# Moving attention weights to their source row by the table's transfer instead of by 0/1 matmuls, in two outlook-attention layers

## The chip, the cores and the metric

The kernel runs on one core of one Trainium2 chip. The metric is the device time of one execution in microseconds; smaller is better. A profile of one execution goes with the times.

## The reference, cut to what matters

Two residual layers over an image batch `x` of shape (8, 56, 56, 384), float32 throughout. Layer 0 normalizes over groups of channels, forms values `v` and, for each pixel, head (12) and each of 9 output offsets `p`, a softmax over 9 input offsets `q`; it weighs the 3x3 neighbourhood of `v` with it, and adds the result for offset `p` onto the pixel at offset `p` (a fold). Layer 1 does the same with 6 heads and no fold.

```python
v_unf = patches.reshape(b, n, k2, heads, d)               # layer 0
attn = jax.nn.softmax(a * d ** (-0.5), axis=-1)           # (b, n, heads, p, q)
out = jnp.einsum('bnhpq,bnqhd->bnphd', attn, v_unf)
canvas = canvas.at[:, i:i + h, j:j + w].add(out[:, :, :, p])
x = x + canvas[:, pad:pad + h, pad:pad + w] @ Wo.T

a = jax.nn.softmax(a.reshape(B, H * W, heads, k * k), axis=-1)   # layer 1
y = jnp.einsum('bpKhd,bphK->bphd', patches, a)
x = x + y @ W_proj + b_proj
```

Seen from a destination pixel, layer 0 is a weighted sum over a 5x5 neighbourhood of source pixels (row offsets -2 to 2), and layer 1 one over a 3x3 neighbourhood. A weight is computed at one pixel's row and is needed at another's.

## The kernel before, in words

A tile has one image column of two images on its partitions: 112 rows (`R`). A pair of images is walked column by column, 4 pairs of 56 columns, so 224 steps in layer 0. Eight groups (`px`) of seven columns make a pair.

Layer 0, one step. `attend` multiplies one column of the normalized input `xn` by the attention weights `wa_t` (three `bank` tiles of 288 columns on TensorE), takes the maximum and subtracts on VectorE (L550, L551), takes Exp on ScalarE (L555), sums on VectorE (L567 to L573), and multiplies by the reciprocal on POOL (L574). A fourth `bank` tile makes `v`, which ScalarE copies (L562) and sends to a table in HBM, `vtab` (L317). `presum`, two steps later, adds on POOL (L593 to L597) the weights of neighbouring columns that meet at one source column, into `pre`. `fold`, three steps later, moves them between rows: `pre` has nine blocks (destination offset `pi` by source offset `qi`), and row offset e from 0 to 4 gathers those with e = pi + 2 - qi. For `qi` = 0 and 2 it multiplies by a 0/1 matrix, `shift`, of TensorE, into `pw`; ScalarE copies the rows e = 0 and 4, to which only one block contributes (L619), VectorE adds the block `qi` = 1, which stays in its row, to e = 1 to 3 (L620), both into the tile `wt`. One or two DMAs of ScalarE's queue (L625), one for each `px` group that the column belongs to, write `wt` to a table in HBM, `ztab`. Its lines are the rows; a line has a slot for each column, and in a slot five pieces of `ROW0` = 84 numbers, one for each e, with zeros around them.

For each group, `bands` reads `ztab` back on SP's queue into `z` (L329), in the form of matrices that a contraction needs, `rows_to_patches` reads `vtab` into `vp`, `contract` multiplies the two (`pc`), ScalarE copies `pc` to `yT` (L664), and `project_out` multiplies by `wo_t` (`po`).

Layer 1 goes by groups of seven columns, 32 in all. `wc_t` makes logits and values in one `bank` tile of 438 columns. The logits go out to a table and come back by rows, `weigh` and `share` make the softmax, and `move` shifts it between rows with three 0/1 matmuls of 126 columns (`pw1`, named `pw` in the profile), nine ScalarE copies into `wz` and one DMA to `ztab1`. `fetch` reads four pieces of `z`, then two of `vp`, on SP's queue, for contractions three steps later.

The order on each engine is partly fixed by the code (a wrapper keeps TensorE, SP, POOL and all of layer 1 in program order); in layer 0 a scheduler orders ScalarE and VectorE. In both layers `jobs` holds contractions and projections, and hands one out between matmuls of the step. [...]

The matrix `inside` holds ones, with zeros at the rows whose neighbour lies in another image.

Of the kernel before, what the change touches and what calls it, by code (L numbers as in the profile page):

```python
# [8 lines left out]
F32 = mybir.dt.float32  # L9
AF = mybir.ActivationFunctionType  # L10
# [5 lines left out]
def two_outlook_layers(  # L16
# [32 lines left out]
    nc = tc.nc  # L49
# [5 lines left out]
    R = IMG * H  # L55
    MARGIN = 2
# [8 lines left out]
    PX = 7  # L65
    NPX = W // PX
# [3 lines left out]
    HEADS0, HEADS1 = 12, 6  # L70
    D0, D1 = C // HEADS0, C // HEADS1
    K, K2 = 3, 9
    E0 = 2 * K - 1
# [9 lines left out]
    ROW0 = HEADS0 * PX  # L83
    WT = 2 * SX0 - E0
    PY1, NPY1, SX1, SY1 = 8, 7, PX + 2, 10
    ROW1 = HEADS1 * PX
# [8 lines left out]
    EP1, FIRST1 = 11, 4  # L95
    SLOT0, SLOT1 = EP0 * ROW0, EP1 * ROW1
    LINE0, LINE1 = SX0 * SLOT0 + ROW0, SX1 * SLOT1 + ROW1
    NTAB = 3
# [11 lines left out]
    ztab0 = [dram.tile([RT + 1, LINE0], F32, name=f"ztab0_{n}") for n in range(NTAB)]  # L110
# [7 lines left out]
    def matmul(*args, **kwargs):  # L118
        tc.keep_in_program_order(nc.tensor.matmul(*args, **kwargs))  # L119
# [48 lines left out]
    shift = const.tile([R, K, R], F32, name="shift")  # L168
    gpsimd.memset(shift, 0.0)
    for k in range(-1, 2):  # L170
        s = shift[:, k + 1, :]
# [10 lines left out]
    inside = const.tile([R, K, PH_ALL], F32, name="inside")  # L182
# [12 lines left out]
    def fill(table, first, dims, width):  # L195

        src = zeros[: dims[0][1], :width]
        if len(dims) > 1:
            src = src.unsqueeze(1).to_broadcast([dims[0][1], dims[1][1], width])
        tc.keep_in_program_order(  # L200
            nc.sync.dma_start(bass.AP(table.tensor, table.offset + first, [*dims, [1, width]]), src)
        )
# [12 lines left out]
    def clear_weights(table, line, part, sx, slot, row, first, e, ep):  # L215
        fill(table, 0, [[part, MARGIN * line // part]], part)
        fill(table, (MARGIN + R) * line, [[part, (MARGIN + 1) * line // part]], part)
        top = MARGIN * line
        fill(table, top, [[line, R]], first * row)
        fill(table, top + (first + e) * row, [[line, R], [slot, sx]], (ep - e) * row)  # L220

    def clears():

        yield 3, lambda: clear_v(vtab0, SX0, 2)

        yield 4, lambda: fill(
            ztab0[0], MARGIN * LINE0 + FIRST0 * ROW0, [[LINE0, R], [SLOT0, 2]], E0 * ROW0
        )
        for n, t in enumerate(ztab0):
            yield (5, 2 * PX, 3 * PX)[n], lambda t=t: clear_weights(  # L230
                t, LINE0, 366, SX0, SLOT0, ROW0, FIRST0, E0, EP0
            )
        yield 4 * PX, lambda: clear_v(vtab1, SX1, 1)
        for n, t in enumerate(ztab1):
            yield (5 + n) * PX, lambda t=t: clear_weights(
                t, LINE1, 350, SX1, SLOT1, ROW1, FIRST1, K, EP1
            )
# [59 lines left out]
    def patches_of(col, pad):  # L297

        for px in range(NPX):
            sx = col - PX * px + pad  # L300
            if 0 <= sx < PX + 2 * pad:
                yield px, sx
# [51 lines left out]
    ps = ctx.enter_context(tc.tile_pool(name="ps", bufs=1, space=PS))  # L354
# [42 lines left out]
    def layer0(late, pools):  # L397
# [209 lines left out]
        def fold(pair, c):  # L607


            pre = pres.pop((pair, c)).rearrange("r (pi qi) f h -> r pi qi (f h)", qi=K)  # L610
            pw = ps.tile([R, E0, E0 * HEADS0], F32, tag="f", name=f"pw_{pair}_{c}")
            for qi in (0, 2):
                matmul(
                    pw[:, 2 - qi : 2 - qi + K, :], shift[:, qi, :], pre[:, :, qi, :],
                    start=(qi == 0), stop=(qi == 2), skip_group_check=True,
                )
            wt = wts[c % NWT]
            mid = wt[:, :, SX0 - E0 : SX0, :].rearrange("r e f h -> r e (f h)")
            nc.scalar.copy(mid[:, 0 : E0 : E0 - 1, :], pw[:, 0 : E0 : E0 - 1, :])  # L619
            nc.vector.tensor_tensor(mid[:, 1 : 1 + K, :], pw[:, 1 : 1 + K, :], pre[:, :, 1, :], ALU.add)  # L620

            for px, sx in patches_of(c, 2):
                lo = SX0 - 1 - sx
                at = sx * SLOT0 + FIRST0 * ROW0
                nc.scalar.dma_start(  # L625
                    ztab0[(pair * NPX + px) % NTAB][MARGIN : MARGIN + R, at : at + E0 * ROW0].rearrange("r (e w) -> r e w", e=E0),
                    wt[:, :, lo : lo + PX, :].rearrange("r e m h -> r e (m h)"),
                )

        def fetch_v(pair, px):  # L630
# [119 lines left out]
        for step in range(NPAIR * W + LAG):  # L750
            if 2 <= step < NPAIR * W + 2:
                presum(*divmod(step - 2, W))
            todo = [lambda: jobs.run(step, 1)] * 2
            if step >= LAG:
                todo.insert(1, lambda: fold(*divmod(step - LAG, W)))
            between = lambda: todo.pop(0)() if todo else None
            if step < NPAIR * W:
                attend(*divmod(step, W), between)
                upkeep(step)
            while todo:  # L760
                between()

            pair, c = divmod(step - LAG - PX, W)
            if pair >= 0 and c % PX == 0:
                fetch_v(pair, c // PX)
            pair, c = divmod(step - LAG - PX - 1, W)
            if pair >= 0 and c % PX == 0:
                fetch(pair, c // PX, step + 4)
# [15 lines left out]
    def layer1(pools, base, last_of_layer0, late_w):  # L784
        vector, scalar, sync = (InOrder(e) for e in (nc.vector, nc.scalar, nc.sync))
# [53 lines left out]
        NW = SX1 * K * ROW1  # L839
# [68 lines left out]

        def move(g):

            at = lgs.pop(g)

            pw = ps.tile([R, K, PX, K, HEADS1], F32, tag="f", name=f"pw1_{g}")
            for ki in range(K):
                matmul(
                    pw[:, K - 1 - ki].rearrange("r x f h -> r x (f h)"),
                    shift[:, ki, :],
                    at.rearrange("r x (i j) h -> r x i (j h)", j=K)[:, :, ki, :],
                    start=True, stop=True,
                )  # L920

            wz = wzs[g % 2]
            step = K * ROW1 + 1
            for kj in range(K):
                dst = wz[:, kj * K * ROW1 : kj * K * ROW1 + PX * step].rearrange("r (m e) -> r m e", e=step)
                dst = dst[:, :, : K * ROW1].rearrange("r m (e h o) -> r e m h o", e=K, h=HEADS1)
                for e in range(K):
                    scalar.copy(dst[:, e, :, :, 0], pw[:, e, :, kj, :])
            table = ztab1[g % NTAB]
            scalar.dma_start(  # L930
                bass.AP(
                    table.tensor, table.offset + MARGIN * LINE1 + FIRST1 * ROW1,
                    [[LINE1, R], [SLOT1, SX1], [1, K * ROW1]],
                ),
                wz[:, :NW].rearrange("r (s e) -> r s e", s=SX1),
            )

        def fetch(g, due):
            pair, px = divmod(g, NPX)
# [76 lines left out]
        for step in range((NG + 1) * PX):  # L1016
            g, m = divmod(step, PX)
# [3 lines left out]
            read, first, second, moved = (0, 2, 3, 4) if last else (1, 3, 4, 5)  # L1021
# [10 lines left out]
            if g and m == moved:  # L1032
                move(done)
# [69 lines left out]
```

## Time and profile before

| what | value |
|---|---|
| three runs, median (lowest to highest) | 3531.84 us (3530.87 to 3535.32) |
| the profiled execution's own time | 3516.74 us |
| its span, mean granted TensorE clock | 3514.6 us, 0.987 |
| layer 0's steps, first to last `pw` | 82.5 to 2311.5 us |
| layer 1's groups, first to last `pw` | 2392.0 to 3460.3 us |
| busy: TensorE, VectorE, POOL, ScalarE | 98%, 55%, 34%, 33% |
| DMA | 839.34 MB, mean 239 GB/s |

A span goes from the first to the last instruction; the time of the execution has a little around it. A row of the groups by shape reads: line, engine, operation, output<-inputs, shape, how often; then busy time in all, mean of one in ns, the engine's idle time before it and what ended that. The line of a helper stands for all its callers: L119 is every matmul, L132 whatever layer 1 keeps in order. A waits row names who waited, for whom, total us, times, and the longest. A DMA row ends with the median time from issue to landing.

### The profile page before, as it was taken

The page shows a single profiled execution, that of the slowest core. Times are in us where ns is not written, and L with a number is a line of the kernel's source. Part 1 is how long each engine was busy: PE and PEld are TensorE (multiplying, and loading weights), DVE is VectorE, ACT ScalarE, POOL GpSimd, SP SyncE. Part 2 cuts the span into 40 slices and gives each one's busy share as a digit, 9 for nine tenths or more (in the row PEclk, how much of TensorE's full clock was granted, in tenths as well). Part 3 has the DMA queues.
Part 4 walks back from the last instruction along what each step waited for, and adds up shares of the span by engine and source line. Part 5 has one row for each costly group of instructions (what it writes and reads, how often), then busy time and mean ns, then how long its engine had stood idle before and what let it go on. Part 6 is the DMA issues. An engine that isn't in the chain of part 4 may idle for free. (4 is left out here: it accounts for less than half of the span.)

```text
span 3514.6 us, 72311 instructions
## 1 busy us (share of the span) xinstructions
PE 3427.7 (98%) x29014; PEld 2353.0 (67%) x29014; DVE 1935.8 (55%) x4680; ACT 1173.3 (33%) x2727; POOL 1202.1 (34%) x1833
## 2 busy tenths in 40 slices
PE   7899999999999999999999999988999999999998
PEld 5577777777777777777777777655666666666665
DVE  6666666667666676667766666633333333333331
ACT  4333223333333233333322223223434434343432
POOL 2543434434344344344443444331222222221220
PEclk8999999999999999999999999999999999999998
DMA  8999988688886878887757776676878787878775
GB/s 270 286 288 282 275 275 267 212 256 253 279 263 209 272 221 273 259 252 256 236 181 226 245 225 193 222 271 192 226 221 234 217 229 219 243 205 237 216 219 147
DMA packets 672893, 839.34 MB, mean 239 GB/s; under 512 B 302190, under 2 KB 566574, under 8 KB 668462
## 3 DMA queue, kind: packets, MB, share of 16 engines
q1 hardware_dynamic: 321422, 537.46, 47.9%
q10 hardware_dynamic: 323872, 210.54, 22.7%
q0 software_dynamic: 27264, 86.73, 7.5%
q8 instruction: 228, 3.74, 0.5%
q14 instruction: 107, 0.88, 0.1%
HBM read 512.95 MB, written 321.66 MB: 237 GB/s over the span
## 5 line engine op out<-in xcount | busy, mean ns | idle before, releaser
L119 PE MATMUL bank<-wa_t,xn 128*112 128x288 f32 x4032 | 1086.9, 409 | 11.4 <-ACT v L562 7.8
L574 POOL TENSOR_TENSOR at<-at,den 112x972 f32<-112x972 f32 x224 | 504.6, 2253 | 1193.1 <-DVE den L573 1137.8
L119 PEld LDWEIGHTS bank<-wa_t,xn 128*112 128x112 f32 x4032 | 693.4, 177 | 263.7 <-issue 34.3
L119 PE MATMUL po<-yT,wo_t 128*128 128x448 f32 (+1 forms) x2304 | 817.5, 494 | 5.3 <-DVE x1t L685 4.8
L119 PEld LDWEIGHTS po<-yT,wo_t 128*128 128x128 f32 x2304 | 432.8, 191 | 293.5 <-issue 185.4
L119 PE MATMUL pc<-z,vp 121*32 121x49 f32 (+1 forms) x17664 | 487.9, 254 | 25.3 <-DMA vp<-vtab 10.4
L119 PEld LDWEIGHTS pc<-z,vp 121*32 121x32 f32 (+1 forms) x17664 | 441.3, 131 | 103.3 <-issue 79.5
L550 DVE TENSOR_REDUCE mx<-bank 112x36 f32<-112x324 f32 x672 | 327.6, 487 | 310.6 <-PE bank L119 303.7
L317 POOL DMA_DIRECT2D vtab<-v x392 | 213.1, 547 | 825.3 <-DVE v L132 810.4
L119 PE MATMUL bank<-wc_t,xn 128*128 128x438 f32 x1176 | 478.8, 543 | 5.0 <-DMA wo_t<-in_wo 5.0
L119 PE MATMUL bank<-wv_t,xn 128*128 128x384 f32 x1176 | 417.9, 492 | 0.0
L555 ACT ACTIVATE at<-at 112x972 f32<-112x972 f32 x224 | 227.0, 1014 | 344.9 <-DVE at L551 317.6
L551 DVE TENSOR_TENSOR at<-bank,mx 112x324 f32<-112x324 f32 x672 | 328.8, 489 | 21.1 <-DVE mx L550 0.5
L119 PEld LDWEIGHTS bank<-wc_t,xn 128*128 128x128 f32 x1176 | 214.0, 191 | 174.8 <-issue 162.4
L119 PEld LDWEIGHTS bank<-wv_t,xn 128*128 128x128 f32 x1176 | 219.5, 190 | 139.6 <-issue 18.7
L619 ACT COPY wt<-pw 112x120 f32<-112x120 f32 x224 | 58.0, 259 | 654.0 <-PE pw L119 591.2
L597 POOL TENSOR_TENSOR pre<-at,at 112x108 f32<-112x108 f32 (+1 forms) x440 | 238.0, 541 | 110.4 <-DVE wt L620 96.0
L567 DVE TENSOR_TENSOR d<-at 112x432 f32<-112x432 f32 x224 | 141.7, 632 | 204.7 <-ACT at L555 204.7
L132 DVE TENSOR_TENSOR lgt<-bank,ba_t 128x54 f32<-128x54 f32 x196 | 41.7, 213 | 361.3 <-PE bank L119 361.3
L132 DVE SCALAR_TENSOR_TENSOR x1t<-po,bo_t,x1t 128x448 f32<-128x448 f32 (+1 forms) x156 | 97.7, 626 | 248.9 <-PE po L119 248.9
L664 ACT COPY yT<-pc 128x294 f32<-128x294 f32 x256 | 103.4, 407 | 368.9 <-PE pc L119 325.9
L535 ACT ACTIVATE xn<-xin,bias,scale 128x224 f32<-128x224 f32 x336 | 172.9, 566 | 67.2 <-PE bank L119 36.0
(100 smaller groups left out, 2924.6 us busy)
## 6 DMA issues: line engine op xcount, KB each, us to landing
z<-ztab SPq DMA_DIRECT2D x64, 2352.0 KB, 18.0
vp<-vtab SPq DMA_DIRECT2D x64, 1536.0 KB, 8.3
ztab<-wt ACTq DMA_DIRECT2D x336, 183.8 KB, 6.8
vp<-vtab SPq DMA_DIRECT2D x64, 945.0 KB, 12.0
xres<-xT SPq DMA_DIRECT2D x32, 1176.0 KB, 10.1
xin<-xT ACTq DMA_DIRECT2D x54, 672.0 KB, 7.3
z<-ztab SPq DMA_DIRECT2D x128, 258.4 KB, 4.5
x1t<-x SPq DMA_DIRECT2D x26, 1176.0 KB, 19.0
```

The source lines that it names most:

```text
L119: tc.keep_in_program_order(nc.tensor.matmul(*args, **kwargs))
L132: return lambda *args, **kwargs: tc.keep_in_program_order(op(*args, **kwargs))
L317: queue.dma_start(bass.AP(table.tensor, table.offset + first, [[line, rows], [(R + GAP) * line - PX * C, n], [1, C]],), v.unsqueeze(1).to_ ...
L535: nc.scalar.activation(to[:, i, :, rows], xin[:, i, :, rows], AF.Identity, bias=bias[:, i, b : b + 1], scale=scale[:, i, b : b + 1],)
L550: nc.vector.tensor_reduce(mx[:, pi, :], pl.rearrange("r q a -> r a q"), AX.X, ALU.max)
L551: nc.vector.tensor_tensor(at[:, pi], pl, mx[:, pi, :].unsqueeze(1).to_broadcast([R, K2, PH]), ALU.subtract)
L555: nc.scalar.activation(at, at, AF.Exp, scale=SCALE0)
L567: nc.vector.tensor_add(d4, at[:, :, 0:4], at[:, :, 4:8])
L574: nc.gpsimd.tensor_tensor(at, at, den.unsqueeze(2).to_broadcast([R, K, K2, PH]), ALU.mult)
L597: nc.gpsimd.tensor_tensor(dst, terms[0], terms[1], ALU.add)
L619: nc.scalar.copy(mid[:, 0 : E0 : E0 - 1, :], pw[:, 0 : E0 : E0 - 1, :])
L664: nc.scalar.copy(yT[:, :, :, b, rows_of], pc.rearrange("p i n y m -> p i m (n y)"))
```

## The change

Row offsets 0 and 4 of layer 0, and all three of layer 1, are no longer moved by TensorE. ScalarE scales the block in its own row by a column of `inside` (zero where the destination lies outside the image) and writes it to `wt` or `wz`; the DMA to the table adds a whole number of lines to the address, so that it lands on the destination's row. In layer 0 the 0/1 matmuls stay for offsets 1 to 3, where two or three blocks are summed: each takes two blocks instead of three, 120 columns instead of 180. The one DMA of five pieces becomes one of three pieces (offsets 1 to 3) and one of two (0 and 4). In layer 1 the one DMA of 126 numbers a slot becomes three of 42 (`ROW1`). Each table gets two more pieces cleared, in the lines that the shifted writes leave out.

```diff
@@ clear_weights
         fill(table, top + (first + e) * row, [[line, R], [slot, sx]], (ep - e) * row)
+        fill(table, top + first * row, [[slot, sx]], row)
+        fill(table, top + (R - 1) * line + (first + e - 1) * row, [[slot, sx]], row)
@@ fold, layer 0
             for qi in (0, 2):
+                lo = qi // 2
                 matmul(
-                    pw[:, 2 - qi : 2 - qi + K, :], shift[:, qi, :], pre[:, :, qi, :],
+                    pw[:, 2 - qi + lo : 4 - qi + lo, :], shift[:, qi, :], pre[:, lo : lo + 2, qi, :],
                     start=(qi == 0), stop=(qi == 2), skip_group_check=True,
                 )
...
-            nc.scalar.copy(mid[:, 0 : E0 : E0 - 1, :], pw[:, 0 : E0 : E0 - 1, :])
+            for e, pi, qi in ((0, 0, 2), (E0 - 1, 2, 0)):
+                nc.scalar.activation(
+                    mid[:, e, :], pre[:, pi, qi, :], AF.Copy, scale=inside[:, qi, 0:1]
+                )
             nc.vector.tensor_tensor(mid[:, 1 : 1 + K, :], pw[:, 1 : 1 + K, :], pre[:, :, 1, :], ALU.add)
...
                 nc.scalar.dma_start(
-                    ztab0[(pair * NPX + px) % NTAB][MARGIN : MARGIN + R, at : at + E0 * ROW0].rearrange("r (e w) -> r e w", e=E0),
-                    wt[:, :, lo : lo + PX, :].rearrange("r e m h -> r e (m h)"),
+                    bass.AP(table.tensor, first + ROW0, [[LINE0, R], [ROW0, K], [1, ROW0]]),
+                    weights[:, 1 : 1 + K],
+                )
+                nc.scalar.dma_start(
+                    bass.AP(
+                        table.tensor, first + LINE0,
+                        [[LINE0, R], [(E0 - 1) * ROW0 - 2 * LINE0, 2], [1, ROW0]],
+                    ),
+                    weights[:, 0 : E0 : E0 - 1],
                 )
@@ move, layer 1
-            pw = ps.tile([R, K, PX, K, HEADS1], F32, tag="f", name=f"pw1_{g}")
-            for ki in range(K):
-                matmul(
-                    pw[:, K - 1 - ki].rearrange("r x f h -> r x (f h)"),
-                    shift[:, ki, :],
-                    at.rearrange("r x (i j) h -> r x i (j h)", j=K)[:, :, ki, :],
-                    start=True, stop=True,
-                )
+            at = at.rearrange("r x (i j) h -> r i x j h", j=K)
...
-                for e in range(K):
-                    scalar.copy(dst[:, e, :, :, 0], pw[:, e, :, kj, :])
+                for ki in range(K):
+                    scalar.activation(
+                        dst[:, K - 1 - ki, :, :, 0], at[:, ki, :, kj, :], AF.Copy,
+                        scale=inside[:, ki, 0:1] if ki != 1 else 1.0,
+                    )
             table = ztab1[g % NTAB]
-            scalar.dma_start(
-                bass.AP(
-                    table.tensor, table.offset + MARGIN * LINE1 + FIRST1 * ROW1,
-                    [[LINE1, R], [SLOT1, SX1], [1, K * ROW1]],
-                ),
-                wz[:, :NW].rearrange("r (s e) -> r s e", s=SX1),
-            )
+            for e in range(K):
+                scalar.dma_start(
+                    bass.AP(
+                        table.tensor,
+                        table.offset + (MARGIN + 1 - e) * LINE1 + (FIRST1 + e) * ROW1,
+                        [[LINE1, R], [SLOT1, SX1], [1, ROW1]],
+                    ),
+                    wz[:, :NW].rearrange("r (s e w) -> r e s w", s=SX1, e=K)[:, e],
+                )
```

In the built program TensorE has 448 calls of `pw` at 120 columns where it had 448 at 180, and none of `pw1`; ScalarE has 448 scaled copies into `wt` for 224 copies, 288 into `wz` as before, 672 DMAs to `ztab` in layer 0 for 336, and 96 to `ztab1` for 32. The order of TensorE and of SP is otherwise the same, and POOL's nearly so; the scheduler orders ScalarE and VectorE anew in layer 0.

More of the change, by code (lines that the diff above doesn't have):

```diff
@@ L624, in fold @@
                 at = sx * SLOT0 + FIRST0 * ROW0
+                table = ztab0[(pair * NPX + px) % NTAB]
+                first = table.offset + MARGIN * LINE0 + at
+                weights = wt[:, :, lo : lo + PX, :].rearrange("r e m h -> r e (m h)")
                 nc.scalar.dma_start(
-                    ztab0[(pair * NPX + px) % NTAB][MARGIN : MARGIN + R, at : at + E0 * ROW0].rearrange("r (e w) -> r e w", e=E0),
-                    wt[:, :, lo : lo + PX, :].rearrange("r e m h -> r e (m h)"),
+                    bass.AP(table.tensor, first + ROW0, [[LINE0, R], [ROW0, K], [1, ROW0]]),
[7 more added lines that the diff above has]
+                    weights[:, 0 : E0 : E0 - 1],
                 )
```

## The prediction, made before the result was known

> **What bounds the kernel now.** I read the page's busy shares first, then the table by stretches of time, then the groups kept apart by shape, then the timeline around one column of layer 0 and one group of layer 1, and last the DMA issues. The page's shares and slices:
>
> ```profile
> PE 3427.7 (98%) x29014; PEld 2353.0 (67%) x29014; DVE 1935.8 (55%) x4680; ACT 1173.3 (33%) x2727; POOL 1202.1 (34%) x1833
> ...
> PE   7899999999999999999999999988999999999998
> ...
> DMA  8999988688886878887757776676878787878775
> ```
>
> TensorE is the only engine near its limit, in nearly every slice. Two rows of the table by stretches (length; busy us of PE, PEld, DVE, ACT, POOL; clock; DMA share; GB/s) show one late stretch of each layer:
>
> ```profile
> 1500.00:2300.00 800.00, 798.22 (x6985) 567.81 (x6987) 542.01 (x1314) 234.74 (x455) 330.88 (x481) 1.00 0.72 230
> 2430.00:2930.00 500.00, 499.28 (x3797) 311.82 (x3796) 157.79 (x335) 200.79 (x585) 110.89 (x205) 1.00 0.81 225
> ```
>
> PE idles 1.8 of 800 us and 0.7 of 500 us. Busy is not peak, so I set it against streaming: the timeline below shows matmuls that start as far apart as their columns cost, without holes. Hence a microsecond taken from PE's stream in either layer is a microsecond of the run, unless another engine then falls behind. The groups that the change touches, by shape:
>
> ```profile
> L119 PE MATMUL pw<-pre,shift 112*112 112x180 f32 x896 | 174.5, 316 | 10.2 <-POOL pre L595 10.2
> ...
> L619 ACT COPY wt<-pw 112x120 f32<-112x120 f32 x224 | 58.0, 259 | 654.0 <-PE pw L119 591.2 <-DMA vtab<-v 36.2 <-DMA xin<-xT 10.5
> ...
> L119 PE MATMUL pw<-at,shift 112*112 112x126 f32 x192 | 29.7, 290 | 0.0
> ```
>
> The means of 316 and 290 ns hold the pipeline's latency, and do not price a matmul. Starts do:
>
> ```profile
> 1012.04 0.78 PE L119 MATMUL pw<-pre,shift 112*112 112x180 f32 x4
> ...
> 1012.65 1.62 PE L119 MATMUL bank<-wa_t,xn 128*112 128x288 f32 x6
> ...
> 2529.38 0.91 PE L119 MATMUL pw<-at,shift 112*112 112x126 f32 x6
> ...
> 2530.12 0.49 PE L122 MATMUL bank<-ident,x1t 128*112 128x128 f32 x3
> ```
>
> Four instructions from 1012.04 to 1012.65 are 0.61 us, 152 ns each for 180 columns; six from 2529.38 to 2530.01 (the next weight load, PE's next work) are 0.63 us, 105 ns each for 126. Both are 0.84 ns a column.
>
> [...]
>
> **The change, part by part.** Times are against the profiled execution, 3516.7 us (span 3514.6); the median of the runs, 3531.8, is 15.1 us above it, and I carry that over unchanged.
>
> Layer 0, PE. `fold` makes 224 x 2 calls, 896 instructions; each falls from 180 to 120 columns. At 0.84 ns a column that is 101 ns instead of 152: 896 x 51 ns = **46 us** off PE. Could weight loads keep the old spacing? The same 112 x 112 weights already go in at 105 ns in layer 1, so 101 to 105: 42 to 46 us. PE's order is otherwise unchanged.
>
> Layer 1, PE. 192 instructions of 105 ns go: **20 us**. So 62 to 66 us leave PE; I take 66.
>
> Layer 0, ScalarE. One 112x120 copy (259 ns) becomes two 60-column activations with a scale per partition: [...], so +0.3 us a column. ScalarE also issues 336 more table DMAs, 1.5 a column, at 0.35 to 0.6 us (two issues of L625 take 0.95): +0.6 us. That is 0.9 us in a column of 9.95 us (2230 us over 224), on an engine 29% busy in the stretch 1500 to 2300. Its throughput hides it. Its order does not, wholly. The old copy waited for PE's matmul; the new activations wait for POOL's `pre`. And in the new order they stand, in most columns, ahead of the Exp two columns later, while the middle rows' DMA, which waits for VectorE's add, is issued after the next column's activations in 142 of 224 columns. So a ring closes: Exp, VectorE's denominator, POOL's product and `pre`, ScalarE's activations and issues, next Exp. One turn as it runs today:
>
> ```profile
> 1015.43 1.01 ACT L555 ACTIVATE at<-at 112x972 f32<-112x972 f32 x1 [2.32 <-DVE at L551]
> ...
> 1017.03 0.59 DVE L567 TENSOR_TENSOR d<-at 112x432 f32<-112x432 f32 x1
> ...
> 1020.08 2.25 POOL L574 TENSOR_TENSOR at<-at,den 112x972 f32<-112x972 f32 x1 [5.59 <-DVE den L573]
> ...
> 1023.13 0.27 POOL L595 COPY pre<-at 112x108 f32<-112x108 f32 x1
> ...
> 1026.12 1.02 ACT L555 ACTIVATE at<-at 112x972 f32<-112x972 f32 x1 [2.32 <-DVE at L551]
> ```
>
> `pre` is complete at 1023.40 and the next Exp starts at 1026.12: 2.7 us. The new ScalarE work in between is 0.5 us for the pair of activations and about three issues of 0.35, 1.55 us. Over columns 30 to 215, taken one by one from the trace, that gap averages 1.6 us, is under 1.55 in about four of ten, and below zero in two. So Exp often comes one to three microseconds later. Queued behind it are the copies of `v` and `yT`; VectorE's sums wait for it, and PE for VectorE's and ScalarE's release of the three banks. Three banks are some 4 us of PE work, so most of the lateness is absorbed. Bounds: 0 lost, if lateness never exceeds 4 us; or 36 us, if it is carried whole from turn to turn and only what exceeds 4 us stops PE. I take 15 us.
>
> Layer 0, DMA. The packets stay at five of 336 bytes a row, so bytes and packets are unchanged. [...]
>
> ```profile
> z<-ztab SPq DMA_DIRECT2D x64, 2352.0 KB, 18.0
> ...
> ztab<-wt ACTq DMA_DIRECT2D x336, 183.8 KB, 6.8
> ...
> ztab<-wz ACTq DMA_DIRECT2D x32, 496.1 KB, 4.4
> ```
>
> Today ScalarE loses about 95 us to DMA waits of up to 5.5 us and PE hardly notices; I expect 50 to 80 us more there and price it on PE at 3 us (0 to 15). SP's order is the same but for 12 small fills at the tables' clearing: nothing, among fills already there.
>
> Layer 0, VectorE. The add drops its wait for the copy (16.5 us in all) and is no longer: nothing.
>
> Layer 1, the move. Nine copies (0.99 us) become nine activations, six with a scale per partition: [...]. They no longer wait for `pw`, and start 0.4 us earlier. One table DMA becomes three, so the last issue is some 1.2 us later; 63 packets per DMA engine become 189. ScalarE's queue took 25 ns a packet in this stretch (55,408 packets, 8.2% of 16 x 1060 us), so landing is 1.5 (at 17 ns, as for the 216-byte packets of the same queue) to 2.8 us later. SP waits for it with z, and vp and x1t are queued behind z. The first vp lands at 2549.7 and its contraction begins at 2553.9: 4.2 us, less 0.6 that PE gains, less 1.5 to 2.8: 0.8 to 2.1 us left. So nothing, but each microsecond beyond it would cost 31 groups x 1 us.
>
> Sum: 66 - 15 - 3 = 48 us. 3516.7 - 48 = 3468.7; as a median, 3531.8 - 48 = **3484 us**.
>
> **Rivals.** (a) Everything hides, the whole 66 us come: 3466. For it: PE lost some 20 us to ScalarE in all of before. Chance 0.20. (b) Layer 1's table lands 1 us beyond the slack in each group: 31 us back, about 3515. For it: the slack is the thinnest margin in the sum; against it: the packets are smaller as well as more. Chance 0.10. (c) Part of the gain only, from weight loads that hold the spacing at 152 ns in layer 0 or a long ring: 3500 to 3538; against it, the 105 ns. Chance 0.09. (d) Slower: the ring becomes layer 0's bound. Its means today are Exp 1.01, wait 0.32, VectorE 3.71, 0.15, POOL 3.27: 8.46, and 1.55 makes 10.0; 0.2 of semaphore waits makes 10.2 against 9.95: 224 x 0.25 = 56, less layer 1's 20: +36, 3568. It decides from a turn of 10.04 (9.95 + 20/224). Against it: VectorE's 3.71 holds its own waits for PE, which shrink when the ring is late. Chance 0.16. My forecast has 0.45.
>
> **How the numbers follow.** Slower than 3538.9 is (d), 0.16. Within 0.2% (7 us, about what a measurement of this kernel can tell) is most of (c), 0.07. The rest is faster, 0.77. Leaving out the tail of (d) and a few below (a), the range is 3460 to 3542.
>
> **What would show it.** Right: `pw` at 120 columns about 101 ns apart, none in layer 1, PE still over 99% in both stretches, a column near 9.8 us and a group near 33.7. Ring: ScalarE's Exp waiting behind POOL's `pre`, PE idle before `bank` for VectorE or ScalarE. Layer 1 wrong: PE waiting for vp in every group. Wrong altogether: PE busy under 97% in layer 0's stretch.

## The result, and the profile after

The changed kernel takes 3722.9 us as the median of four runs (3719.7 to 3726.2), against 3531.9 before: a ratio of 1.0537, with a 95% interval of 1.0522 to 1.0552. The forecast was 3484, in a range up to 3542. It was wrong in sign, by 239 us.

The page of the execution profiled after, with the engines' shares, the slices and the packets:

```profile
PE 3449.9 (93%) x28822; PEld 2336.1 (63%) x28822; DVE 1914.9 (51%) x4680; ACT 1250.6 (34%) x2951; POOL 1194.9 (32%) x1833
...
PE   7799999999999999999999999789988888898897
...
PEclk7999999999999999999999999999999999899997
DMA  7988887787887698877677776788997988798885
...
DMA packets 744052, 839.44 MB, mean 225 GB/s; under 512 B 373343, under 2 KB 637727, under 8 KB 739615
```

PE fell from 98% of the span to 93%, and the loss stands in the last third of the slices: layer 1. The table by stretches (length; busy us of PE, PEld, DVE, ACT, POOL; clock; DMA share; GB/s) says it more sharply:

```profile
1500.00:2300.00 800.00, 793.35 (x7084) 556.53 (x7083) 542.32 (x1328) 256.89 (x543) 332.81 (x486) 1.00 0.73 234
2430.00:2930.00 500.00, 441.25 (x3241) 273.90 (x3241) 136.69 (x291) 180.69 (x509) 95.90 (x177) 0.94 0.86 188
2930.00:3430.00 500.00, 446.33 (x3160) 275.61 (x3160) 132.84 (x283) 178.85 (x499) 93.76 (x174) 0.92 0.86 188
```

In layer 0's stretch PE runs 7084 instructions where it ran 6985. In layer 1's it is idle for 59 of 500 us where it was idle for 0.7, its clock is 0.94, and the DMA engines are busier (0.86 against 0.81) while they move less (188 GB/s against 225).

Taken apart at the start of layer 0's last Exp (2298.2 before, 2303.6 after), the two profiled executions, 3514.6 and 3724.5 us long, differ by 5 us up to there and by 204 us behind it. A group of layer 1 takes 41.1 us, the median of 27, where it took 34.3.

The groups of instructions that the change touches are as forecast. By shape, and for `pw` as starts in the timeline around one column:

```profile
L626 ACT ACTIVATE wt<-pre,inside 112x60 f32<-112x60 f32 x448 | 133.3, 338 | 797.6 <-POOL pre L598 651.9 <-DMA vtab<-v 71.4 <-DMA ztab<-wt 38.1
L119 PE MATMUL pw<-pre,shift 112*112 112x120 f32 x896 | 130.8, 268 | 18.0 <-POOL pre L598 18.0
...
L132 DVE TENSOR_REDUCE mx<-at 112x42 f32<-112x378 f32 x32 | 26.6, 830 | 331.1 <-DMA at<-lgtab 331.1
```

```profile
1017.63 0.57 PE L119 MATMUL pw<-pre,shift 112*112 112x120 f32 x4
1018.04 1.62 PE L119 MATMUL bank<-wa_t,xn 128*112 128x288 f32 x6
```

Four `pw` from 1017.63 to 1018.04 are 103 ns each, where 101 was worked out. ScalarE now waits for POOL's `pre`, 652 us in all. That alone shows no cost: before, the old copy stood 654 us idle at the same place, most of it for PE's `pw`. What was not foreseen is the last line by shape: VectorE waits 331 us for the logits `at`. Before, it waited 131:

```profile
L132 DVE TENSOR_REDUCE mx<-at 112x42 f32<-112x378 f32 x32 | 26.7, 835 | 130.6 <-DMA at<-lgtab 130.6
```

The timeline of SP's queue in one group shows where these come from. Here the group's three table DMAs were issued at 2927.00, 2927.35 and 2928.02, and by the trace's completions they landed at 2934.87, 2936.28 and 2938.58:

```profile
2938.72 1.88 SPq L132 DMA_DIRECT2D z<-ztab  x4
2940.84 1.04 SPq L132 DMA_DIRECT2D vp<-vtab  x2
2941.97 2.92 SPq L132 DMA_DIRECT2D x1t<-x  x1
2945.00 1.00 SPq L132 DMA_DIRECT2D at<-lgtab  x1
```

The table's last landing starts a train: `z`, `vp`, the next group's `x1t`, and last the logits `at` of the following group, which lands at 2960.86, just behind `x1t` (2960.34). SP's waits in layer 1 (2450 to 3600), first before and then after:

```profile
SPq L132 <- DMA ztab<-wz: 530.9, 30, 25.4
SPq L132 <- DMA lgtab<-lgt: 281.2, 28, 13.8
```

```profile
SPq L132 <- DMA ztab<-wz: 897.8, 28, 35.0
...
SPq L132 <- DMA lgtab<-lgt: 13.3, 7, 4.4
```

Before, SP waited in turn for the table and for the logits' landing in `lgtab`. Now the train is so late that `lgtab` has nearly always landed. So `at` is issued earlier after the change than before, 17.7 us after the group's first table DMA against 21.7 (medians), and still lands later, 16.2 us behind its issue and level with `x1t` (34.0): what it waits for now is the train ahead of it. Before, with the issue so late, this view doesn't tell whether the issue or the train set its landing. And PE's waits over the whole run, after; before, the first was 10.4 us and the second 7.0:

```profile
PE pc L119 <- DMA vp<-vtab: 86.7, 23, 17.5
PE pc L119 <- ACT yT L132: 74.3, 26, 5.9
```

The second line is how late logits reach PE. ScalarE's order is fixed in layer 1, and the copies `yT` that free PE's `pc` stand behind the Exp of the logits, which waits for VectorE's maximum and subtraction. In the group above:

```profile
2962.34 0.52 ACT L132 ACTIVATE at<-at 112x378 f32<-112x378 f32 x1 [8.10 <-DVE at L132]
...
2963.12 0.64 ACT L132 COPY yT<-pc 128x336 f32<-128x336 f32 x2
```

Between 2450 and 3600 PE's `pc` waits for `yT` make 69.1 us, and each of them has such an Exp, late itself, within it or at most 2 us ahead of it.

**The ring.** A ring is a loop of steps of which each waits for the one before; a group can't be shorter than once round it. I took each group's issues and completions from the trace and counted from its first table DMA. Medians over 27 groups, in us:

| kernel | table has landed | first `vp` lands | `at` lands | from `at` to the next table DMA | group |
|---|---|---|---|---|---|
| before | 4.1 | 18.6 | 27.7 | 7.0 | 34.3 |
| after | 10.2 | 25.1 | 33.9 | 6.8 | 41.1 |

From the table's landing to `at`'s it is 23.6 us before and 23.7 after. From there, through the maximum, Exp, the shares and the move, it is 7.0 and 6.8 to the next table DMA. The two legs are as long as before, and only the landing moved, by 6.1 us. The sums are 34.7 and 40.7, against groups of 34.3 and 41.1: this ring was closed before the change, with no slack at all, and level with TensorE's own work. That is a theory from two traces. Its rivals: the queues' throughput, whatever the order; the slower ScalarE; layer 0's added DMAs.

### The profile page after: what moved, and what is told of

Same layout as the page of the kernel before. It is cut to its first block, busy times and chain, and to the rows that moved or that the text cites. A ratio compares the mean times of both kernels' runs of the same rounds, so it can differ in the third digit from the quotient of the medians.

```text
span 3724.5 us, 72630 instructions
## 1 busy us (share of the span) xinstructions
PE 3449.9 (93%) x28822; PEld 2336.1 (63%) x28822; DVE 1914.9 (51%) x4680; ACT 1250.6 (34%) x2951; POOL 1194.9 (32%) x1833
## 5 line engine op out<-in xcount | busy, mean ns | idle before, releaser
L119 PE MATMUL bank<-wa_t,xn 128*112 128x288 f32 x4032 | 1086.7, 409 | 14.3 <-ACT v L565 10.8
L119 PEld LDWEIGHTS bank<-wa_t,xn 128*112 128x112 f32 x4032 | 682.1, 177 | 268.3 <-issue 33.5
L119 PE MATMUL pc<-z,vp 121*32 121x49 f32 (+1 forms) x17664 | 521.5, 261 | 177.3 <-DMA vp<-vtab 86.7
L119 PEld LDWEIGHTS pc<-z,vp 121*32 121x32 f32 (+1 forms) x17664 | 472.9, 137 | 259.4 <-issue 94.1
L119 PE MATMUL bank<-wc_t,xn 128*128 128x438 f32 x1176 | 518.3, 580 | 4.7 <-ACT xn L132 4.7
L626 ACT ACTIVATE wt<-pre,inside 112x60 f32<-112x60 f32 x448 | 133.3, 338 | 797.6 <-POOL pre L598 651.9
L119 PEld LDWEIGHTS bank<-wc_t,xn 128*128 128x128 f32 x1176 | 230.1, 206 | 195.9 <-issue 178.7
L554 DVE TENSOR_TENSOR at<-bank,mx 112x324 f32<-112x324 f32 x672 | 327.6, 487 | 21.2 <-DVE mx L553 0.5
L119 PEld LDWEIGHTS bank<-wv_t,xn 128*128 128x128 f32 x1176 | 217.1, 190 | 160.9 <-DVE at L554 25.4
L132 DVE TENSOR_REDUCE mx<-at 112x42 f32<-112x378 f32 x32 | 26.6, 830 | 331.1 <-DMA at<-lgtab 331.1
```

Source lines behind the costliest of these rows:

```text
L132: return lambda *args, **kwargs: tc.keep_in_program_order(op(*args, **kwargs))
L554: nc.vector.tensor_tensor(at[:, pi], pl, mx[:, pi, :].unsqueeze(1).to_broadcast([R, K2, PH]), ALU.subtract)
L626: nc.scalar.activation(mid[:, e, :], pre[:, pi, qi, :], AF.Copy, scale=inside[:, qi, 0:1])
```

## The experiments

All times are given as ratios to the kernel before on the same chip, where it took 3538 to 3540 us; a thousandth is 3.5 us.

### Each half alone

`l0_only` has the new `fold`, with its two fills a table, and the old `move`; `l1_only` the reverse. No line differs from the diff above.

> Layer 0's part alone (the narrower 0/1 matmuls, edge rows by two activations, two table DMAs a patch), layer 1 as before. Theory A (the loss is layer 1's, and layer 0's own gain is lost again inside layer 0): in the kernel after, layer 0's last pw matmul stands at 2316.9 us against 2311.5 before, so this one lands within 10 us of before, 3522 to 3542. Theory B (layer 0's 46 us of PE time do come, and are hidden by what layer 1 does): 3485 to 3500. In either case a layer-1 group is back to 34.3 us.

> Layer 1's part alone (nine activations and three table DMAs, no 0/1 matmuls there), layer 0 as before. Theory A: layer 1's group period goes from 34.3 to about 40.5 us, and the whole loss is there: 3531 + 31 x 6.2 = about 3720. Theory B (layer 0's extra table DMAs or its late end disturb layer 1 too, through the queues or the clock): clearly under 3690.

Measured: layer 0's part **0.9965** (0.9948 to 0.9983), 3525.9 us; layer 1's part **1.0612** (1.0594 to 1.0629), 3753.0 us. So the whole loss is layer 1's, about 213 us, and layer 0's part is a gain of some 12 us. Theory A holds for both, though layer 0's gain is a little over the 10 us that it allowed and layer 1's part cost more than the 190 that it expected. The two parts add up to 201 us where the whole change costs 190; this difference was not followed.

### Layer 1: the pieces, the number of DMAs, ScalarE

Three kernels take the move apart. `after_one_dma` puts one DMA of 504-byte pieces back behind the new activations:

```diff
-            for e in range(K):
-                scalar.dma_start(...[[LINE1, R], [SLOT1, SX1], [1, ROW1]]...)   # 168-byte pieces
+            scalar.dma_start(...[[LINE1, R], [SLOT1, SX1], [1, K * ROW1]]...)   # 504-byte pieces
```

> The kernel after with layer 1's three table DMAs put back into one of 504-byte pieces; the nine activations from at stay, no 0/1 matmuls. What is left out: layer 1's row offset (rows go to the table unshifted), so the output differs. Theory A (three DMAs of 168-byte pieces land late: 11.6 us from first issue to last landing against 4.4): the landing is back near 4.5 to 5, the ring is 34 to 35 us, and the time 3530 to 3560. Theory B (what delays is ScalarE: nine activations of 1.87 us against 0.99, and its order): the period stays over 39 us and the time over 3680.

`before_three_dmas` makes the opposite edit in the kernel before: three DMAs, one for each e, in place of one, all to the old addresses.

> The kernel before with layer 1's one table DMA of 504-byte pieces cut into three of 168-byte pieces; the 0/1 matmuls and the nine copies stay, and the rows go where they went. Theory A (the small pieces alone make the table late): the last landing goes from 4.1 to about 10 us after the first issue, the group's period from 34.3 to 39.5 to 40.5 us, and the time rises by 160 to 190 us. Theory B (the small pieces hurt only together with the slower activations and the missing matmuls): less than 80 us more than before.

`before_three_big` has three DMAs too, cut the other way, so that the pieces stay whole:

```diff
-            scalar.dma_start(...[[LINE1, R], [SLOT1, SX1], [1, K * ROW1]]...)
+            for n in range(0, SX1, 3):
+                scalar.dma_start(...[[LINE1, R], [SLOT1, 3], [1, K * ROW1]]...)
```

> The kernel before with layer 1's one table DMA cut into three by groups of three slots, so that there are three DMAs and the pieces stay 504 bytes. Theory A (the number of pieces makes the table late): two more issues put the last landing 0.6 to 1.5 us later, 4.7 to 5.6 us against 10.8 with 168-byte pieces, and the time is at most 45 us over before. Theory B (three DMAs with their issues and their completions make it late): 150 us or more over before.

| kernel | ratio (95%) | table has landed | `at` lands | to the next table DMA | group |
|---|---|---|---|---|---|
| `after_one_dma` | 1.0065 (1.0049 to 1.0082) | 4.7 | 28.5 | 7.4 | 35.7 |
| `before_three_dmas` | 1.0616 (1.0591 to 1.0641) | 10.8 | 34.9 | 6.6 | 41.8 |
| `before_three_big` | 1.0015 (1.0005 to 1.0026) | 4.8 | 28.3 | 6.3 | 35.0 |

The small pieces alone, with the 0/1 matmuls and the copies still there, cost all of it and a little over what A expected (218 us against 160 to 190). Three DMAs of whole pieces cost 5 us. The activations in place of the matmuls, with whole pieces, leave 23 us over before. As layer 0 gains 12, layer 1 loses about 35 us even so. Its ring is 35.9 us long (28.5 + 7.4) where that of `before_three_big` is 34.6, and PE waits 29.7 us for `yT` between 2450 and 3430 where it waits 12.0 there. The nine operations of ScalarE take 1.86 us instead of 0.99, which is the likely reason but was not tested alone; the 20 us of PE work that are gone don't shorten the ring.

What a piece costs, from the pages of `before_three_dmas` and `before_three_big` (ScalarE's queue; packets, MB, share of 16 engines) and their DMA issues (KB each, median us from issue to landing):

```profile
q10 hardware_dynamic: 389408, 210.54, 25.4%
...
ztab<-wz ACTq DMA_DIRECT2D x96, 165.4 KB, 9.3
```

```profile
q10 hardware_dynamic: 324896, 210.54, 23.2%
...
ztab<-wz ACTq DMA_DIRECT2D x96, 165.4 KB, 4.1
```

Same bytes, same number of DMAs, 64,512 more packets. The shares are 15,264 and 13,129 us (25.4% of 16 x 3755.8, 23.2% of 16 x 3536.9), and so an added packet costs 33 ns, though it adds no byte; the mean over that queue is 40 ns with 648 bytes. The packet records of the two traces, 2430 to 3430, show it directly: a piece of 504 bytes took 29.6 ns on average, and one of 168 bytes 31.3. A table is 63 packets on each engine with whole pieces and 189 with small ones: 126 x 33 ns = 4.2 us of the 6.0 by which its landing moved between these two kernels.

### Layer 1: is it the order of SP's queue?

If the ring closes only because SP issues in order, an order that keeps `at` and `vp` from standing behind the table must open it. `after_read_first` exchanges `read_logits(done)` and `load(g + 1)`, so that `at` goes ahead of `x1t`.

> The kernel after with two lines of layer 1 exchanged: the logits' read (at<-lgtab) is issued on SP ahead of the next group's x1t instead of behind it. Theory A (a ring sets the group's period: at lands, max, Exp, share and the nine activations 6.6 us, three table DMAs land 11.6 us, SP issues z, vp, x1t and at 6.3 us, at lands behind x1t 16 us, together 40.5): x1t's 1.2 MB are some 5 us at the stretch's 225 GB/s, so at lands 4 to 6 us earlier, the period falls to about 35 to 36.5, and the time to 3560 to 3610. Theory B (the DMA queues' throughput with three times the small packets sets the period, whatever the order): within 15 us of the kernel after, 3710 to 3738.

`after_at_pool` takes `at` off SP altogether; the second kernel also moves `vp` ahead of `z`:

```diff
-            sync.dma_start(lgs[g]...)          # read_logits
+            nc.gpsimd.dma_start(lgs[g]...)
...
-            for b in range(IMG): bands(sync, zs1[...], ztab1[g % NTAB], ...)
             for b in range(IMG): rows_to_patches(sync, vps[b], vtab1, ...)
+            for b in range(IMG): bands(sync, zs1[...], ztab1[g % NTAB], ...)
```

> The kernel after with the logits' read (at<-lgtab) issued on GpSimd's queue instead of SP's, so that it stands behind none of z, vp and x1t. Theory A (the loss is a ring that closes through SP's order): at lands about 5 us after lgtab's landing, near 21 us after the group's first wz issue instead of 34; the ring at to wz to z to at is gone, and what is left is vp's landing, at 25 us against 18.6 before with 4.2 us of slack there: 2.3 us late a group, 71 us, less 20 us of PE work: 50 us over before plus layer 0's change, 3560 to 3610. Theory B (the DMA engines can't carry the small pieces, in any order): 3690 or more.

> As the run with at on GpSimd's queue, and vp's two reads are issued on SP ahead of z's, so that they no longer wait for the weights' table. Theory A: vp crosses while the table lands, z alone is left behind the landing, and nothing in layer 1 waits for the small pieces any more; the period falls to 33.7 to 35 us, the time to 3500 to 3550. Theory B (throughput, not order): no more than 15 us better than with at on GpSimd's queue alone.

| kernel | ratio (95%) | table has landed | first `vp` lands | `at` lands | to the next table DMA | group |
|---|---|---|---|---|---|---|
| `after_read_first` | 1.0433 (1.0417 to 1.0448) | 10.7 | 25.9 | 31.4 | 8.2 | 39.8 |
| `after_at_pool` | 1.0484 (1.0463 to 1.0504) | 10.6 | 26.8 | 24.9 | 16.1 | 40.9 |
| `after_at_pool_vp_first` | 1.0131 (1.0103 to 1.0159) | 17.2 | 15.4 | 28.5 | 7.5 | 36.8 |

In the third kernel SP has mostly issued one of the pair's two `vp` reads ahead of the table DMA (it lands at 1.6 us); 15.4 is then the other.

The first two missed what A expected, by 80 and 100 us. The first is nonetheless 37 us better than the kernel after, by the ratios, and fits neither forecast; the second fell on B's side of 3690 (3711.4 us). With `at` on another queue it lands 9 us earlier, is no longer urgent (16.1 us to the next table DMA), and the group hardly moves. The waits of PE and of VectorE in that kernel, 2450 to 3600, name what binds instead:

```profile
PE pc L119 <- DMA vp<-vtab: 92.4, 23, 7.5
```

```profile
DVE mx L132 <- DMA at<-lgtab: 51.9, 24, 4.5
```

VectorE's wait for `at` is down from 285 us in the same stretch of the kernel after, and PE's wait for `vp` is up from 56. So there are **two rings** of nearly one length, and both go through the table's landing and SP's order: one by `at`, the other by `vp` and the contraction, 26.8 us to the first `vp` and the other 14.1 of the group's 40.9 to the next table DMA. That the second binds is read from PE's waits here, and tested by the next kernel. Opening one of them brings little.

A wait of PE cost more than its length here. The timeline of PE around one group's first contraction, first before, then in `after_at_pool`, and the latter's clock in 2917 to 2921 (0.50, the third value from the right):

```profile
2934.35 1.61 PE L119 MATMUL pc<-z,vp 90*64 90x56 f32 x48
2935.89 2.47 PE L119 MATMUL bank<-wc_t,xn 128*128 128x438 f32 x6
```

```profile
2916.39 2.82 PE L119 MATMUL pc<-z,vp 90*64 90x56 f32 x48 [2.73 <-DMA vp<-vtab]
2919.14 4.26 PE L119 MATMUL bank<-wc_t,xn 128*128 128x438 f32 x6
```

```profile
2917.00:2921.00 4.00, 4.00 (x45) 3.11 (x43) 0.00 (x0) 1.29 (x3) 0.00 (x0) 0.50 1.01 304
```

With a wait of 2.7 us the clock falls to 0.50, for 6.8 us by the trace's clock records (2915.9 to 2922.7), and the same 54 instructions take 6.8 us instead of 3.9, start to start. In the next group a wait of 1.9 us was followed by 0.50 for 3.4 us. The leg from the first contraction to the next table DMA, a median of 11.7 us before, is 14.2 here.

This group is one of the worse ones. Over 2450 to 3600 PE idles 118 us in `after_at_pool` and 131 in the kernel after, and what the clock withholds while PE works comes to 75 and 73 us more: about 0.6 us for each us of waiting. For the kernel after that adds up: 131 + 73 less the 18 us of `pw1` work that is gone, over 28 groups, is 6.6 us a group (an estimate from these sums), and 6.8 were lost.

With both opened the same view of PE gives `vp` no line, and 4 short waits for `z`:

```profile
PE pc L119 <- DMA z<-ztab: 2.8, 4, 1.2
```

The small pieces are as many as before, and now share the engines with `vp`, so that the table lands at 17.2 us. Still the run is 127 us shorter than with `at` moved alone. So the order carries most of the loss, and theory B falls, though A expected 34 to 84 us more than came. What is left, 36.8 a group, may be once more a ring by `at` (28.5 + 7.5 = 36.0), which is issued at 19.8, when `lgtab` has landed (19.1); PE's longest waits are again for `yT`. No run tested this, and the engines, busy 0.94 of the time between 2500 and 3400 (0.78 in `after_one_dma`), may have a part in it. This kernel still loses to the kernel before.

### Layer 0: where 46 us became 12

At first the trace seemed to put a loss of 20 us into the first 35 columns, and I put it down to the added fills. `l0_fills_pool` issues those on GpSimd's queue:

> Layer 0's part alone, with the six fills that it adds for clearing (two a table) issued on GpSimd's queue instead of SP's. Layer 0's part alone had lost 20 us to before by column 35 and won 20 us back from column 50 to 223. Theory A (the added fills hold up SP's in-order queue, and with it z and vp, while the tables are cleared): the early loss shrinks to under 10 us, and the time falls by 8 to 15 us against layer 0's part alone, to a ratio of 0.992 to 0.994 with before. Theory B (the early loss is the ring over ScalarE, or the doubled table DMAs where the DMA engines are 0.9 busy): within 4 us of layer 0's part alone, a ratio of 0.995 to 0.998.

Measured: 0.9970 (0.9960 to 0.9980); theory B. The reading was faulty at its root: it compared with a trace from another chip. `before_three_big`, whose layer 0 is the old one, reaches column 50 at 561.8 us where the kernel before had reached it at 554.0. On the chip of `l0_only` itself, an old layer 0 (`l1_only`) is there at 567.7, and `l0_only` at 568.5. But the other six traces with the new layer 0 on these three chips are there 1 to 14 us later than the old one on their chip, so that a loss ahead of column 50 is likely; its size and cause stay open. So only the rest is compared from here on, columns 50 to 223, where four traces with the old layer 0 agree: 1744.1, 1746.0, 1746.3 and 1746.3 us.

Two kernels take the new layer 0 apart. `l0_one_dma` goes back to one table DMA a patch, `l0_no_edges` then drops the two activations as well:

```diff
-                nc.scalar.dma_start(..., weights[:, 1 : 1 + K])
-                nc.scalar.dma_start(..., weights[:, 0 : E0 : E0 - 1])
+                nc.scalar.dma_start(ztab0[...][...], wt[:, :, lo : lo + PX, :]...)
...
-            for e, pi, qi in ((0, 0, 2), (E0 - 1, 2, 0)):                      # l0_no_edges only
-                nc.scalar.activation(mid[:, e, :], pre[:, pi, qi, :], AF.Copy, scale=...)
```

> Layer 0's part alone, but with one table DMA a patch as before; the narrower matmuls and the two edge activations stay. What is left out: the edge rows' shift, so the output differs. Layer 0's part alone had a ratio of 0.9965 with before. Theory A (the early loss of some 20 us and half of the later gain go to the 336 added table DMAs): 0.989 to 0.993. Theory B (they go to ScalarE's two activations and their wait for POOL's pre, the ring): 0.995 to 0.998.

> As the run with one table DMA, and the two edge activations are left out too; what stays is the narrower matmul. Left out are thus the edge rows of layer 0's weights. This is the ceiling of what PE's 46 us can bring: ScalarE has less to do than before (no 259 ns copy). Both theories: a ratio of 0.986 to 0.990 if a microsecond off PE's stream is a microsecond of the run; a ratio over 0.993 would say that the loss is neither of the two, and that PE's saved columns are not all time.

| kernel | ratio (95%) | columns 50 to 223 |
|---|---|---|
| old layer 0 (four traces) | | 1744 to 1746 |
| `l0_only` | 0.9965 (0.9948 to 0.9983) | 1728.2 |
| `l0_one_dma` | 0.9917 (0.9893 to 0.9941) | 1720.1 |
| `l0_no_edges` | 0.9909 (0.9893 to 0.9925) | 1709.6 |

The stretch 500 to 2300 of the last three, and ahead of them of `before_three_big` with the old layer 0:

```profile
500.00:2300.00 1800.00, 1796.41 (x15973) 1284.27 (x15963) 1228.11 (x3024) 553.00 (x1082) 733.16 (x1065) 1.00 0.78 241
```

```profile
500.00:2300.00 1800.00, 1783.11 (x16240) 1259.38 (x16238) 1230.31 (x3062) 605.06 (x1274) 740.37 (x1079) 1.00 0.77 244
```

```profile
500.00:2300.00 1800.00, 1783.85 (x16331) 1264.14 (x16330) 1225.43 (x3050) 606.60 (x1273) 739.95 (x1079) 1.00 0.80 245
```

```profile
500.00:2300.00 1800.00, 1791.12 (x16553) 1271.49 (x16551) 1236.26 (x3068) 516.01 (x920) 749.60 (x1085) 1.00 0.79 246
```

The narrower matmul alone brings all its columns here: 173 columns of 0.204 us are 35 us, and 1745.7 - 1709.6 = 36. That holds in this stretch only; the whole of `l0_no_edges` gains 32 us, not 46. Up to column 50 it gains nothing that can be seen (569.2 us, where `before_three_big` has 561.8 on the same chip). With the edges and the DMAs, PE idles 17 us of 1800 instead of 4, and half of the 36 us is lost. By the ratios the added DMAs cost 17 us over the run (0.9965 against 0.9917, intervals 0.0007 apart, each against before on its own chip), and the activations with their ring 3 us, which the intervals don't resolve; by the stretch the two cost 8 and 10.5 us. PE idles as long in `l0_one_dma` as in `l0_only` (16 and 17 us), so the 8 us between these two are not seen as idle time. Since the same layer 0 took 1728 to 1737 us in eight traces, how the loss divides between them stays open.

### A version that beats both

`l0_best` is `l0_only` with the two new orders in the old layer 1: `at` on GpSimd's queue and `vp` ahead of `z`.

> Layer 0's part alone, with layer 1 as before but for two orders: the logits' read on GpSimd's queue, and vp's reads on SP ahead of z's. Theory A (layer 1's ring of 34.7 us through SP's queue is its bound in layer 0's part alone, where PE idles some 4 of 500 us): the group's period falls to 34.2 to 34.4 and the ratio to 0.991 to 0.994. Theory B (layer 1 is PE's already): within 4 us of layer 0's part alone, 0.9955 to 0.998.

Measured: **0.9899** (0.9879 to 0.9919), 3501.7 us, the fastest of the kernels that leave nothing out. The stretch 2430 to 3430, first of `l0_only`, then of this kernel:

```profile
2430.00:3430.00 1000.00, 992.18 (x7648) 620.99 (x7648) 315.60 (x669) 396.87 (x1159) 221.38 (x407) 1.00 0.80 223
```

```profile
2430.00:3430.00 1000.00, 1000.00 (x7759) 627.21 (x7758) 318.73 (x673) 402.75 (x1169) 250.38 (x441) 1.00 0.81 224
```

PE has no idle time left in this stretch, and the median group falls from 34.7 to 34.3 us with the same work on PE. From layer 0's last Exp to the end it is 1199.6 us, against 1225.0, and 1228.6 in `l0_no_edges`, which ran on the same chip. `at` is issued as late as ever (21.6 us after the table DMA; 21.2 in `l0_only`), but without the train ahead of it it lands 3.4 us behind its issue instead of 6.8. So the two orders bring some 25 us in the old layer 1 as well. 8 of them are PE's idle time in the stretch, which fits the ring. About 7 more come at layer 1's first contraction, ahead of the stretch, where PE waits 11.8 us for `vp` in `l0_only` and 4.8 for `z` here; the rest was not located.

## Why the prediction was wrong

**What bounds the kernel: half right.** That a microsecond off PE is one of the run held for layer 0 from column 50 on. It was not seen in the first 50 columns, at which I had not looked apart: of the 46 us, the narrower matmul alone brought 32 over the run. It failed for layer 1 in a way that the view could not show: PE idle for 0.7 of 500 us proves that PE is a bound, not that it is the only one. The ring of 34.7 us was level with it. Removing 20 us of PE's work there could bring next to nothing, and any delay in the ring came through in full.

**Layer 0, PE: right** (103 ns measured against 101; 36 us of 35 in the stretch). **ScalarE's ring and its added waits for DMAs, 15 + 3 us: right in the sum alone**, some 18 us of the stretch's 35, and 20 over the run by the ratios (0.9965 against 0.9909). That the sum fits is partly luck: the added DMAs, which I priced at 3 us, cost 8 by the stretch and 17 by the ratios, the activations 10.5 and 3. Both prices rested in part on estimates of mine that no trace then showed. I put a pair of activations at 0.5 us, or +0.3 us a column (two at the old copy's 259 ns would be 0.52); measured in the kernel after, it is 0.58 us from the first's start to the second's end, a median. And I put ScalarE's added waits for DMAs at 50 to 80 us; up to 2300 us they went from 97 us before to 260 after. The fills at nothing: no cost of them was found. Rival (d), the slower one, was the wrong place: the ring in layer 0 never became the bound.

**Layer 1, ScalarE: right.** The 1.8 us for nine activations were an estimate of mine, for a form of activation that the trace before does not show; 1.86 was measured, from the first start to the last end. One by one they took 356 and 263 ns with and without an operand of one value a partition (medians), which makes 2.93 us for the nine, so they overlapped by 1.07.

**Layer 1, the table's landing: the step that failed.** It was to be 1.5 to 2.8 us later, behind issues 1.2 us later, with "0.8 to 2.1 us left". Measured: 6.1 us later in all. The packets were counted rightly (63 to 189 an engine). But even at the forecast's own 17 to 25 ns the 126 added ones make 2.1 to 3.2 us, and 3.3 to 4.4 together with the 1.2 us of issues; 1.5 to 2.8 doesn't come out of its figures. And they were priced too low, from a queue's average over a stretch and from pieces of 216 bytes: an added piece cost 33 ns. The remaining 2 us are not taken apart; the last issue is 1.0 us behind the first, and the pieces share engines that are busy 0.86 of the time. "against it: the packets are smaller as well as more" was the mistake put into words: I let the size count, and here the two sizes took nearly the same, 31.3 ns at 168 bytes and 29.6 at 504.

**The slack: right in size, and the second step that failed.** From the first `vp` to its contraction the median was 4.5 us before (I had 4.2) and is 0.1 after. But I took it for the price of the whole delay. By that reckoning, 6.1 us less a slack of 3.6 cost 31 x 2.5 = 78 us (an estimate), while layer 1 lost some 200. Two things were missing. SP's order also puts `at` behind the table, and that loop had no slack: I asked what is queued behind SP's wait, and named `vp` and `x1t`, but not the read behind them, whose consumer leads to the next table DMA. And a wait of PE, once there, cost more than half as much again in clock (about 0.6 us for each us, over 2450 to 3600). By `vp` alone, with `at` freed, the group was 40.9 us. Rival (b), at a chance of 0.10, came nearest: it had the landing beyond the slack and the price of a microsecond (31 us for 31 groups), but not the loop by `at`; 6.8 of them came, not 1.

## What to carry to other kernels

An engine that is 99.9% busy may still run level with a loop through a queue: follow each transfer that is moved to its own next issue, add up the loop, and compare it with the period before pricing a delay at nothing. Price a DMA by its pieces and not by its bytes: here the same bytes in pieces cut in three made the table land 6.0 us later (10.8 against 4.8, with three DMAs both times). On a queue that the program keeps in order, as SP's here, issue what doesn't need the late data ahead of what does. Where two loops share the late transfer, reorder for both: here one alone brought 19 us, and both 144 of the 190 that were lost.

## What was not expected of the hardware

An added 168-byte piece cost 33 ns of a DMA engine, and a piece took about as long at 168 bytes (31.3 ns) as at 504 (29.6); in the kernels after and before, over the same stretch, it was 27.0 and 30.0. Issuing took longer too: of a group's three table DMAs in the kernel after, the first holds ScalarE's queue for 311 ns, as before, the second for 591 and the third for 918 (medians), so that three take 1.8 us and not 0.9. With whole pieces, in `before_three_big`, it is 312, 506 and 526. And PE's clock fell to 0.50 with waits of 1.9 and 2.7 us in `after_at_pool`, so that over layer 1 a microsecond of waiting cost about 1.6.
